# The last stage of a four-layer decoder block, the mixture of LoRA experts, as a written-out pipeline over tiles

## The chip, the cores and the metric

The kernel runs on one core of one Trainium2 chip, in one launch. The metric is the device time of an execution in microseconds (us), taken from the first to the last thing that the core does. Five engines work on it, each through its own queue of instructions: PE (TensorE, matrix products and transposes; its weight loads are listed as PEld), DVE (VectorE), ACT (ScalarE), POOL (GpSimd) and SP (SyncE, which issues most DMAs).

## What is computed

Sixteen sequences of 128 tokens with 256 channels pass through four layers. Each layer adds a gated cross attention (or a long convolution in layer 0) and then a gated feed-forward part to `x`. The change concerns the last of these eight parts, and touches the end of the one before:

```python
x = x + tanh(g_xattn[3]) * L3_xattn(layernorm(x), ctx)     # attention, 16 heads of 8
x = x + tanh(g_ffn[3])   * L3_ffn(layernorm(x))            # mixture of LoRA experts

def L3_ffn(x):                               # x: 2048 tokens x 256
    probs = softmax(x @ Wr.T + br)           # 8 experts
    expert_idx, expert_weight = argmax(probs), max(probs)
    h = einsum('nd,erd->ner', x, A)          # rank 64 for each expert
    y = einsum('ner,eor->neo', h, B) / 64
    return y[n, expert_idx] * expert_weight
```

The kernel computes `h` of all eight experts at once (8 x 64 = 512 columns), multiplies each expert's 64 columns by its gate (the probability of the best expert over 64, and zero for the seven others), and takes one product with all of `B`.

## The kernel before

`x` stays in SBUF as four tiles `xg[0..3]` of four sequences each (128 tokens on the partitions, 4 x 256 columns). A sequence is called a tile below, b = 0 to 15, and four of them are a group. The stages follow one another in `passage`, lines 1738 to 1789; each opens its own buffer pools.

Most instructions are put in order by a planner (the Tile framework), which may weave instructions of the next stage into the one before where their inputs allow. A stage under `tc.manual_schedule(engines=...)` keeps PE, DVE and ACT instructions in the order in which the program text issues them; POOL and SP follow the planner.

`stage_l3x` (the attention of layer 3, from line 1386) is such a stage: a pipeline of eight steps for a tile. On PE a tile has eight products `s` (L1568), four products `av` (L1584), eight transposes `ta` (L1600), two `tt` (L1615), the output product `y` (L1626), and for a later tile the projections `qk` (L1461, L1462) and `tv` (L1506). ACT takes the exponentials `pt` of `s` (L1575) and the scaled output `ys` (L1631). POOL adds `ys` to `x` (L1633), and for a later tile gathers two rows for each token (`yc`, L769) and takes the reciprocal root `rs` of the variance (L1443). DVE copies `av` out of PSUM (`avs`, L1595), normalises (L1607, L1610), copies `tt` (L1620), adds the gathered rows to `x` (L1432) and takes its statistics. The earlier tiles have gathers and projections for later tiles beside their own work; the last ones have none.

The softmaxes of the two attention layers are taken without subtracting a maximum. To guard this, `sums_seen` (L63, L64) keeps the largest and smallest reciprocal of a sum in `inv`. `verdict` (L66 to L80) reduces these on DVE (L70 to L73), sums over the partitions with one small PE product (L76), and writes `flag` (L78 to L80). Every engine loads the flag at the end (L48) and jumps over a second passage of the whole program, which takes the maxima and isn't executed with these inputs. `verdict` is called ahead of `stage_l3f`, with a PSUM pool of its own.

`stage_l3f` (line 1695) is left to the planner. For each group g it calls

- `layernorm` (L151): `bn_stats` and `bn_aggr` of each of four tiles on DVE (`st`, L157; `mv`, L158), `ve` (L160), the power -0.5 on POOL (`rs`, L162), and four DVE instructions `xn` (L165). The planner placed most of these statistics in `stage_l3x`, each behind the `x` of L1633 that it reads.
- `transposed` (L168): eight PE transposes (L174), the halves copied by DVE and by ACT (`xnT`, L175).
- `logits` (L343): eight small products `lg` (L347) and the addition of the bias (`l`, L354); `exp_shifted` (L357): the maximum (`mx`), the difference (`ex`, L362) and the exponential on ACT (L363).
- the sum (L1705), its reciprocal, and `topk_mask` (L327): for each pair of experts it compares "greater" (L332) and "equal" (L334), breaks ties by a constant triangle `tri` (L336), adds (L337), sums over the pairs (L339) and compares with k - 0.5 (L340). With k = 1 this marks the first of the largest. Three more instructions make `gate` (L1708 to L1710).

and then for each of the group's four tiles: `ph` (L1714, two products of 512 columns), `hid` = `ph` x `gate` on DVE (L1722), four transposes of `hid` (L1726), their copy `hT` on ACT (L1728), four products `y` (L1731), and `x` + tanh(g) x `y` on DVE (L1733). One DMA stores the group (L1734). A product of 32-bit floats is two PE instructions (passes) in the profile; a transpose is one.

Of the kernel before, what the change touches and what calls it, by code (L numbers as in the profile page):

```python
# [10 lines left out]
F32 = mybir.dt.float32  # L11
BF16 = mybir.dt.bfloat16
F32R = mybir.dt.float32r
AF = mybir.ActivationFunctionType
ALU = mybir.AluOpType
AX = mybir.AxisListType
PSUM = bass.MemoryType.PSUM

P = 128
B = 16  # L20
D = 256
NG = 4
# [33 lines left out]
def passage(ctx: ExitStack, tc: tile.TileContext, a: dict, out: bass.AP, inv, flag):  # L56
# [6 lines left out]
            nc.vector.tensor_tensor(inv[:, 0, n], inv[:, 0, n], rc, ALU.max)  # L63
            nc.vector.tensor_tensor(inv[:, 1, n], inv[:, 1, n], rc, ALU.min)  # L64

    def verdict():  # L66

        with tc.tile_pool(name="vd", bufs=1) as vd, tc.tile_pool(name="vdp", bufs=1, space=PSUM) as ps:
            m = vd.tile([P, 2, 2], F32, name="m")
            nc.vector.tensor_reduce(m[:, 0], inv[:, 0], AX.X, ALU.max)  # L70
            nc.vector.tensor_reduce(m[:, 1], inv[:, 1], AX.X, ALU.min)
            nc.vector.tensor_scalar(m[:, 0], m[:, 0], 1e20, None, ALU.is_gt)
            nc.vector.tensor_scalar(m[:, 1], m[:, 1], 1e-30, None, ALU.is_lt)  # L73
            m = m.rearrange("p a b -> p (a b)")
            t = ps.tile([1, 4], F32, name="t")
            nc.tensor.matmul(t, lhsT=ones[:, 0:1], rhs=m, start=True, stop=True)  # L76
            f = vd.tile([1, 1], F32, name="f")
            nc.vector.tensor_reduce(f, t, AX.X, ALU.max)  # L78
            nc.vector.tensor_scalar(f, f, 0.5, None, ALU.is_gt)
            nc.vector.tensor_copy(flag, f)  # L80
# [70 lines left out]
    def layernorm(pool, g, extra=None, tag="xn"):  # L151
# [12 lines left out]
        for k in range(GB):  # L164
            nc.vector.tensor_scalar(xn[:, k, :], x[:, k, :], mv[:, k, 0:1], rs[:, k : k + 1], ALU.subtract, ALU.mult)  # L165
        return xn

    def transposed(pool, ps, xn, tag="xnT"):  # L168

        xT = pool.tile([P, 2, GB * P], F32, name="xnT", tag=tag)  # L170
        for c in range(2):
            t = ps.tile([P, GB * P], F32, name="tp", tag="tp")
            for k in range(GB):
                nc.tensor.transpose(t[:, k * P : (k + 1) * P], xn[:, k, c * P : (c + 1) * P], ident)  # L174
            (nc.scalar.copy if c else nc.vector.tensor_copy)(xT[:, c, :], t)  # L175
        return xT

    def bc(ap, axis, n):

# [32 lines left out]
    def stage_l0x(ka, vbuf, anyk):  # L212

        with tc.tile_pool(name="s0", bufs=1) as s0, tc.tile_pool(name="s0w", bufs=2) as s0w, tc.tile_pool(
# [103 lines left out]
            for b in range(0, B, 2):  # L318
# [3 lines left out]
                        nc.tensor.transpose(t[:, (2 * k + c) * P : (2 * k + c + 1) * P], oT[:, c, b + k, :], ident)  # L322
                xv = xg[b // GB][:, b % GB : b % GB + 2, :].rearrange("p b d -> p (b d)")
                nc.vector.scalar_tensor_tensor(xv, t, tg[:, 0:1], xv, ALU.mult, ALU.add)


    def topk_mask(v, k, pool):  # L327

        n = v.shape[1]
        mine, other = bc(v, 3, E), bc(v, 2, E)  # L330
        gt = pool.tile([P, n, E, E], F32, name="gt", bufs=1)
        nc.vector.tensor_tensor(gt, other, mine, ALU.is_gt)  # L332
        eq = pool.tile([P, n, E, E], F32, name="eq", bufs=1)
        nc.vector.tensor_tensor(eq, other, mine, ALU.is_equal)  # L334
        f = "p t a b -> p t (a b)"
        nc.vector.tensor_tensor(eq.rearrange(f), eq.rearrange(f), bc(tri, 1, n), ALU.mult)  # L336
        nc.vector.tensor_tensor(gt.rearrange(f), gt.rearrange(f), eq.rearrange(f), ALU.add)  # L337
        m = pool.tile([P, n, E], F32, name="m")
        nc.vector.tensor_reduce(m, gt, AX.X, ALU.add)  # L339
        nc.vector.tensor_scalar(m, m, k - 0.5, None, ALU.is_lt)  # L340
        return m

    def logits(ps, xT, gw, bias=None):  # L343
        lg = ps.tile([P, GB, E], F32, name="lg", tag="tp")
        for k in range(GB):
            for c in range(2):
                nc.tensor.matmul(  # L347
                    lg[:, k, :], lhsT=xT[:, c, k * P : (k + 1) * P], rhs=gw[:, c, :], start=(c == 0), stop=(c == 1)
                )
        l = small.tile([P, GB, E], F32, name="l")  # L350
        if bias is None:
            nc.vector.tensor_copy(l, lg)
        else:
            nc.vector.tensor_tensor(l, lg, bc(bias, 1, GB), ALU.add)  # L354
        return l

    def exp_shifted(l):  # L357

        mx = small.tile([P, GB], F32, name="mx")
        nc.vector.tensor_reduce(mx, l, AX.X, ALU.max)  # L360
        ex = small.tile([P, GB, E], F32, name="ex")
        nc.vector.tensor_tensor(ex, l, bc(mx, 2, E), ALU.subtract)  # L362
        nc.scalar.activation(ex, ex, AF.Exp)  # L363
        return ex


    def moe0_weights():
# [1325 lines left out]


    def stage_l3f(wa, wb, wr, br):
        with tc.tile_pool(name="lo", bufs=2) as lo, tc.tile_pool(name="lot", bufs=2, space=PSUM) as pst, tc.tile_pool(
            name="lou", bufs=2, space=PSUM
        ) as psu:
            for g in range(NG):
                xn = layernorm(lo, g)  # L1700
                xT = transposed(lo, pst, xn)
                ex = exp_shifted(logits(pst, xT, wr, br))

                s = small.tile([P, GB], F32, name="s")
                nc.vector.tensor_reduce(s, ex, AX.X, ALU.add)  # L1705
                nc.vector.reciprocal(s, s)
                gate = small.tile([P, GB, E], F32, name="gate")
                nc.vector.tensor_tensor(gate, ex, topk_mask(ex, 1, lo), ALU.mult)  # L1708
                nc.vector.tensor_tensor(gate, gate, bc(s, 2, E), ALU.mult)
                nc.vector.tensor_scalar(gate, gate, 1.0 / 64.0, None, ALU.mult)  # L1710
                for k in range(GB):
                    ph = psu.tile([P, E, 64], F32, name="ph")
                    for c in range(2):
                        nc.tensor.matmul(  # L1714
                            ph.rearrange("p e r -> p (e r)"),
                            lhsT=xT[:, c, k * P : (k + 1) * P],
                            rhs=wa[:, c, :],
                            start=(c == 0),
                            stop=(c == 1),
                        )  # L1720
                    hid = lo.tile([P, E, 64], F32, name="hid")
                    nc.vector.tensor_tensor(hid, ph, bc(gate[:, k, :], 2, 64), ALU.mult)  # L1722
                    t = pst.tile([P, 4, P], F32, name="tp")
                    hf = hid.rearrange("p e r -> p (e r)")
                    for i in range(4):
                        nc.tensor.transpose(t[:, i, :], hf[:, i * P : (i + 1) * P], ident)  # L1726
                    hT = lo.tile([P, 4, P], F32, name="hT")
                    nc.scalar.copy(hT, t)  # L1728
                    y = psu.tile([P, D], F32, name="y")
                    for i in range(4):  # L1730
                        nc.tensor.matmul(y, lhsT=hT[:, i, :], rhs=wb[:, i, :], start=(i == 0), stop=(i == 3))  # L1731
                    xv = xg[g][:, k, :]
                    nc.vector.scalar_tensor_tensor(xv, y, tg[:, 7:8], xv, ALU.mult, ALU.add)  # L1733
                nc.sync.dma_start(out[g * GB : (g + 1) * GB].rearrange("b p d -> p b d"), xg[g])  # L1734

# [45 lines left out]
    with tc.tile_pool(name="l3fw", bufs=1) as fw:  # L1783
        l3a = col_chunks("l3a", a["L3_A"], 512, fw)
        l3B = col_chunks("l3B", a["L3_B"], D, fw)
        stage_l3x(*l3w, pos, wgt, ys)
        if not search:
            verdict()
        stage_l3f(l3a, l3B, l3r, l3br)


# [88 lines left out]
```

## Time and profile before

| | us |
|---|---|
| median of 3 runs | 1131.65 |
| lowest and highest run | 1130.06, 1133.9 |
| the profiled execution's own time | 1133.69 |
| its span, from the first to the last instruction | 1132.0 |
| PE busy in the span | 928.8 (82%) |
| DVE busy | 637.4 (56%) |
| ACT busy | 413.7 (37%) |
| POOL busy | 329.2 (29%) |
| mean granted PE clock | 0.877 |

A busy PE is not PE at its peak: where the granted clock is 0.5, the same products take twice the time. The page cuts the span into 40 slices of 28.3 us; the last four hold the end of `stage_l3x` and all of `stage_l3f`. The timeline lists instructions with start, length, engine, line, operation and names; what stands in brackets is how long the engine was idle before, and what ended that. The chain of waits is followed back from the last instruction to what released each step.

### The profile page before, as it was taken

To read this page: it belongs to the slowest core of one execution; us is meant where nothing else is said; L and a number is where in the kernel's file an instruction comes from. 1 tells how busy PE (TensorE), PEld (TensorE's weight loads), DVE (VectorE), ACT (ScalarE), POOL (GpSimd) and SP (SyncE) were. 2 spreads that over 40 slices of the span, in tenths; PEclk is the share of its full clock that TensorE was granted. 3 is DMA by queue.
4 is the path that set the end of the run, shared out by engine and by line. 5 is a ranking of instruction groups with operands and counts; after the bars stand their busy time and mean duration, and the time that the engine had idled before them with its cause. 6 is when DMAs were issued, how large, how long until landed. Compare 5 with 4: busy or idle time off the path is not lost. (4 is left out here: it accounts for less than half of the span.)

```text
span 1132.0 us, 14992 instructions
## 1 busy us (share of the span) xinstructions
PE 928.8 (82%) x5216; PEld 602.4 (53%) x5216; DVE 637.4 (56%) x1641; ACT 413.7 (37%) x674; POOL 329.2 (29%) x343
## 2 busy tenths in 40 slices
PE   3899798899998999936673658799269999998886
PEld 1444376677786454423331558688145555555563
DVE  5988847222235555389779859344245556535432
ACT  2110043233223444413331133355257777881110
POOL 5766223543034251000001117551443342210000
PEclk9999989999998999958665557899569999997998
DMA  9100170334113059000000101343388777520010
GB/s 303 26 0 1 30 198 1 93 107 100 55 56 98 29 95 116 1 29 0 1 1 0 56 19 53 97 149 95 119 234 243 201 213 197 164 66 1 19 37 22
DMA packets 71322, 94.12 MB, mean 83 GB/s; under 512 B 9191, under 2 KB 63047, under 8 KB 68935
## 3 DMA queue, kind: packets, MB, share of 16 engines
q1 hardware_dynamic: 55544, 64.98, 19.4%
q0 software_dynamic: 14080, 23.78, 10.4%
q10 hardware_dynamic: 1616, 4.33, 1.1%
q8 instruction: 45, 0.74, 0.3%
q14 instruction: 37, 0.30, 0.1%
HBM read 57.06 MB, written 33.55 MB: 80 GB/s over the span
## 5 line engine op out<-in xcount | busy, mean ns | idle before, releaser
L1575 ACT ACTIVATE pt<-s 128x1024 f32<-128x1024 f32 x128 | 126.4, 1023 | 36.7 <-PE s L1568 34.2
L769 POOL DMA_INDIRECT yc<-ys,pos x64 | 62.0, 968 | 125.9 <-DVE x L788 51.3
L309 PE MATMUL y<-kv,toep 128*128 128x512 f32 x192 | 86.7, 603 | 1.5 <-DVE toep L249 1.5
L1568 PE MATMUL s<-qa,ka 64*128 64x256 f32 x512 | 64.8, 334 | 7.3 <-ACT pt L1575 6.2
L1584 PE MATMUL av<-pt,v 128*32 128x256 f32 x1024 | 69.4, 389 | 0.1
L301 POOL TENSOR_TENSOR kv<-ctxT 128x1024 f32<-128x1024 f32 x32 | 60.1, 1899 | 28.5 <-PE y L309 28.5
L162 POOL TENSOR_TENSOR rs<-ve,neghalf 128x4 f32<-128x4 f32 x16 | 16.3, 1016 | 172.9 <-DVE ve L160 136.5
L1568 PEld LDWEIGHTS s<-qa,ka 64*128 64x128 f32 x512 | 39.0, 190 | 45.9 <-issue 24.2
L309 PEld LDWEIGHTS y<-kv,toep 128*128 128x128 f32 x192 | 35.7, 192 | 43.6 <-issue 40.2
L157 DVE BATCH_NORM_STATS2 st<-x 128x6 f32<-128x256 f32 x64 | 26.1, 415 | 52.4 <-POOL x L1633 39.8
L676 PE MATMUL ub<-L0we,xbT 128*128 x160 | 52.2, 470 | 2.6 <-ACT xbT L667 2.6
L972 PE MATMUL yb<-L2we,hT 88*128 (+1 forms) x224 | 43.0, 322 | 10.3 <-issue 4.0
L653 POOL DMA_INDIRECT xb<-xs,who x40 | 38.1, 951 | 44.9 <-PE tb L665 34.2
L907 POOL DMA_INDIRECT xb<-xs,who x40 | 38.1, 952 | 32.3 <-PE tb L919 21.0
L314 DVE TENSOR_TENSOR pr<-y,qT 128x1024 f32<-128x1024 f32 x32 | 39.0, 1222 | 12.3 <-PE y L309 9.4
L1595 DVE COPY avs<-av 128x256 f32<-128x256 f32 x64 | 26.7, 417 | 30.9 <-PE av L1584 30.7
L972 PEld LDWEIGHTS yb<-L2we,hT 88*128 88x128 f32 x224 | 34.9, 213 | 17.2 <-DVE hT L796 8.9
L537 PE MATMUL up<-L0s,xT 128*128 128x352 f32 x128 | 43.3, 484 | 0.0
L1475 POOL TENSOR_TENSOR hl<-f,hl 128x512 fp32r<-128x512 f32 x16 | 20.5, 1280 | 77.6 <-ACT hl L1474 77.6
L1147 ACT ACTIVATE pt<-s 128x1024 f32<-128x1024 f32 x32 | 32.7, 1023 | 25.4 <-PE s L1144 25.3
L317 DVE TENSOR_REDUCE oT<-pr 128x128 f32<-128x1024 f32 x32 | 38.9, 1219 | 1.0
L676 PEld LDWEIGHTS ub<-L0we,xbT 128*128 128x128 f32 x160 | 29.6, 195 | 16.2 <-ACT xbT L667 2.8
(382 smaller groups left out, 2071.6 us busy)
## 6 DMA issues: line engine op xcount, KB each, us to landing
scr<-hl SPq DMA_DIRECT2D x64, 256.0 KB
ys<-ysb SPq DMA_DIRECT2D x40, 256.0 KB
qa<-scr SPq DMA_DIRECT2D x32, 256.0 KB
ka<-scr SPq DMA_DIRECT2D x32, 256.0 KB
L2we<-in_L_w_dram POOLq DMA_DIRECT2D x6, 792.0 KB
L0we<-in_L_w_dram SPq DMA_DIRECT2D x6, 704.0 KB
xs<-xn SPq DMA_DIRECT2D x8, 512.0 KB
x<-in_x_dram SPq DMA_DIRECT2D x4, 512.0 KB
```

Of the source, the lines that this page charges most:

```text
L301: nc.gpsimd.tensor_tensor(t, bc(ch, 3, 8), bc(ch, 2, 8), ALU.mult)
L309: nc.tensor.matmul(y[:, ns], lhsT=T[:, h, d : d + P], rhs=kv[mc][:, ns], start=(mc == 0), stop=(mc == lc))
L314: nc.vector.tensor_tensor(pr, y.rearrange("p (b j i) -> p b j i", b=B, j=8), bc(qT[:, lc, :, hs], 2, 8), ALU.mult)
L317: nc.vector.tensor_reduce(oT[:, lc, :, hs], pr, AX.X, ALU.add)
L537: nc.tensor.matmul(t[:, n, 0 : 2 * I], lhsT=xT[:, c, b * P : (b + 1) * P], rhs=s13[:, c, n, :], start=(c == 0), stop=(c == 1),)
L653: nc.gpsimd.indirect_dma_start(out=xbs[s][:, i, :], out_offset=None, in_=xs, in_offset=bass.IndirectOffsetOnAxis(ap=who[:, 2 * s + i : 2 * ...
L676: nc.tensor.matmul(t[:, i, 0 : 2 * I], lhsT=xbT[:, i, c, :], rhs=we[:, bass.ds(regs[s][i] + c * 2 * I, 2 * I)], start=(c == 0), stop=(c == 1),
L769: nc.gpsimd.indirect_dma_start(out=got[b][:, i, :], out_offset=None, in_=ys, in_offset=bass.IndirectOffsetOnAxis(ap=pos[:, i, b : b + 1], ...
L972: nc.tensor.matmul(y[:, i, :], lhsT=hT[:, x, k, i, :], rhs=we[0:HI, bass.ds(at[i] + 4 * I + k * D, D)], start=(n == 0), stop=(n == 3),)
L1568: nc.tensor.matmul(s[:, h, jj, :], lhsT=ka[r, 2 * i + jj, sc * P : (sc + 1) * P], rhs=qa[r, 2 * i + jj, :], start=True, stop=True,)
L1575: nc.scalar.activation(pts[b, i][:, sc], s, AF.Exp)
L1584: nc.tensor.matmul(av[c : c + 32, :], lhsT=va[:, sc, 8 * h + 2 * i + jj, :], rhs=pt[:, sc, h, jj, :], start=(sc == 0), stop=(sc == 1),)
```

## The change

`stage_l3f` is written anew under `tc.manual_schedule`, as a pipeline with one step for each tile; its functions are issued at fixed distances ahead of the tile n of a step (`group(f, ahead)` issues once per group). The helpers `transposed`, `topk_mask`, `logits` and `exp_shifted` go. Both copies of the transposed `x` are on ACT. The mask of the best expert is now a comparison with the maximum, a running sum of the result that starts anew at every token (`tensor_tensor_scan` with `anew`, which is 0 at each first expert and 1 elsewhere), and a comparison of that sum with 1. The PSUM pools have four buffers for all but `ph`, and three for `ph`. `verdict` is called inside, in the step n = 4, and takes a PSUM buffer of the stage. `x` is stored in pairs of tiles, and the last two tiles singly.

```diff
-    def verdict():
-        with tc.tile_pool(name="vd", bufs=1) as vd, tc.tile_pool(name="vdp", bufs=1, space=PSUM) as ps:
+    def verdict(ps):
+        with tc.tile_pool(name="vd", bufs=1) as vd:
...
-            t = ps.tile([1, 4], F32, name="t")
+            t = ps.tile([1, 4], F32, name="tv", tag="a")
...
     def stage_l3f(wa, wb, wr, br):
-        with tc.tile_pool(name="lo", bufs=2) as lo, tc.tile_pool(name="lot", bufs=2, space=PSUM) as pst, tc.tile_pool(
-            name="lou", bufs=2, space=PSUM
-        ) as psu:
-            for g in range(NG):
...
+        with tc.tile_pool(name="lo", bufs=2) as lo, tc.tile_pool(name="lot", bufs=4, space=PSUM) as pst, tc.tile_pool(
+            name="lou", bufs=3, space=PSUM
+        ) as psu, tc.manual_schedule(
+            engines={mybir.EngineType.PE, mybir.EngineType.DVE, mybir.EngineType.Activation}
+        ):
+            anew = lo.tile([P, GB, E], F32, name="anew", bufs=1)
+            nc.gpsimd.memset(anew, 1.0)
+            nc.gpsimd.memset(anew[:, :, 0:1], 0.0)
...
+            def stats(g):
...
+                for k in range(GB):
+                    nc.vector.bn_stats(st[:, k, :], xg[g][:, k, :])
+                    nc.vector.bn_aggr(mv[:, k, :], st[:, k, :])
+                ve = lo.tile([P, GB], F32, name="ve")
+                nc.vector.tensor_scalar_add(ve, mv[:, :, 1], LN_EPS)
+                rs = lo.tile([P, GB], F32, name="rs")
+                nc.gpsimd.tensor_tensor(rs, ve, neghalf, ALU.pow)
+                mvs[g] = mv, rs
+
+            def normal(g):
...
+            def turn(g):
+                xn = xns.pop(g)
+                xTs[g] = lo.tile([P, 2, GB * P], F32, name="xT")
+                for c in range(2):
+                    t = pst.tile([P, GB * P], F32, name="tx", tag="a")
+                    for k in range(GB):
+                        nc.tensor.transpose(t[:, k * P : (k + 1) * P], xn[:, k, c * P : (c + 1) * P], ident)
+                    nc.scalar.copy(xTs[g][:, c, :], t)
...
+            def likely(g):
...
+                nc.vector.tensor_tensor(l, lgs.pop(g), bc(br, 1, GB), ALU.add)
...
+                nc.vector.tensor_reduce(mx, l, AX.X, ALU.max)
...
+                nc.vector.tensor_tensor(ex, l, bc(mx, 2, E), ALU.subtract)
+                nc.scalar.activation(ex, ex, AF.Exp)
+
+            def chosen(g):
...
+                nc.vector.tensor_reduce(s[:, 0], ex, AX.X, ALU.add)
+                nc.vector.tensor_reduce(s[:, 1], ex, AX.X, ALU.max)
+                nc.vector.reciprocal(s[:, 0], s[:, 0])
...
+                nc.vector.tensor_tensor(eq, ex, bc(s[:, 1], 2, E), ALU.is_equal)
...
+                nc.vector.tensor_tensor_scan(
+                    cum.rearrange(f), anew.rearrange(f), eq.rearrange(f), 0.0, ALU.mult, ALU.add
+                )
+                nc.vector.scalar_tensor_tensor(eq, cum, 1.0, eq, ALU.is_equal, ALU.mult)
+                nc.vector.tensor_tensor(ex, ex, eq, ALU.mult)
...
+                nc.vector.scalar_tensor_tensor(gate, ex, 1.0 / 64.0, bc(s[:, 0], 2, E), ALU.mult, ALU.mult)
...
+            def turn_hidden(b):
+                hf = hids.pop(b).rearrange("p e r -> p (e r)")
+                t = pst.tile([P, 4, P], F32, name="th", tag="a")
+                for i in range(4):
+                    nc.tensor.transpose(t[:, i, :], hf[:, i * P : (i + 1) * P], ident)
+                hTs[b] = lo.tile([P, 4, P], F32, name="hT")
+                nc.scalar.copy(hTs[b], t)
+
+            def down(b):
...
+                y = pst.tile([P, D], F32, name="y", tag="a")
+                for i in range(4):
+                    nc.tensor.matmul(y, lhsT=hT[:, i, :], rhs=wb[:, i, :], start=(i == 0), stop=(i == 3))
+                xv = xg[g][:, k, :]
+                nc.vector.scalar_tensor_tensor(xv, y, tg[:, 7:8], xv, ALU.mult, ALU.add)
+                if b >= B - 2:
+                    nc.sync.dma_start(out[b], xv)
+                elif k % 2:
+                    nc.sync.dma_start(out[b - 1 : b + 1].rearrange("b p d -> p b d"), xg[g][:, k - 1 : k + 1, :])
...
+            for n in range(-4, B + 2):
+
+                def group(f, ahead):
+                    g, r = divmod(n + ahead, GB)
+                    if r == 0:
+                        when(f, g, NG)
+
+                when(down, n - 2)
+                group(turn, 2)
+                group(logit, 1)
+                when(up, n)
+                when(turn_hidden, n - 1)
+                group(likely, 1)
+                group(stats, 4)
+                group(normal, 3)
+                group(chosen, 0)
+                when(gated, n)
+                if n == GB and not search:
+                    verdict(pst)
...
         stage_l3x(*l3w, pos, wgt, ys)
-        if not search:
-            verdict()
         stage_l3f(l3a, l3B, l3r, l3br)
```

`logit`, `up` and `gated` hold the same products and the same multiplication as the lines L347, L1714 and L1722 before, for one group or one tile. On PE the built program has, in a step of the steady state: `y`(n-2), the transposes `tx` or the logits `lg` of a coming group where one is due, `ph`(n), `th`(n-1), and in the step n = 4 the product `tv` of the check.

## The prediction

> **What bounds the kernel now.** I read the page's slices first, then the chain of waits in the two stages that the change can reach, then the timeline of the last one. Only the end of the span is concerned: `stage_l3x` (about 832 to 1024 us) and `stage_l3f` (1024 us to the end).
>
> ```profile
> span 1132.0 us, 14992 instructions
> ...
> PE   3899798899998999936673658799269999998886
> ...
> PEclk9999989999998999958665557899569999997998
> ```
>
> The last four slices, `stage_l3f`, read 8886 on PE: it is the bound there, with holes. The stage in one row (columns: stretch, its length, then busy time of PE, PE's weight loads, DVE, ACT and POOL, clock, DMA share, GB/s):
>
> ```profile
> 1024.00:1125.44 101.44, 87.44 (x352) 58.09 (x352) 41.23 (x115) 12.62 (x24) 1.75 (x2) 0.89 0.05 16
> ```
>
> PE is busy for 87.4 of 101.4 us, at 0.89 of its clock. The timeline gives the price of each piece of one tile, read from start to start:
>
> ```profile
> 1092.32 0.60 PE L1726 MATMUL tp<-ident,hid 128*128 128x128 f32 x4
> ...
> 1092.76 1.02 PE L1714 MATMUL ph<-l3a,xnT 128*128 128x512 f32 x2
> 1093.01 0.58 ACT L1728 COPY hT<-tp 128x512 f32<-128x512 f32 x1 [2.58 <-PE tp L1726]
> ...
> 1093.65 1.99 PE L1731 MATMUL y<-l3B,hT 128*128 128x256 f32 x8
> ...
> 1095.48 1.02 PE L1714 MATMUL ph<-l3a,xnT 128*128 128x512 f32 x2
> ```
>
> Four transposes take 0.44 us, half a `ph` (2 passes) 0.86, so a whole one 1.72, and `y` 1.83. From the first transpose to `y` it is 1.33 us, because `y` needs ACT's copy `hT`. The 0.86 of `ph` between them hides nearly all of that. Once per group the gates are late:
>
> ```profile
> 1055.17 0.19 DVE L354 TENSOR_TENSOR l<-lg,l3br 128x32 f32<-128x32 f32 x1 [0.74 <-PE lg L347]
> ...
> 1059.38 1.29 DVE L1722 TENSOR_TENSOR hid<-ph,gate 128x512 f32<-128x512 f32 x2
> 1060.13 0.42 PEld L1726 LDWEIGHTS tp<-ident,hid 128*128 128x128 f32 x4 [3.15 <-DVE hid L1722]
> 1060.13 0.66 PE L1726 MATMUL tp<-ident,hid 128*128 128x128 f32 x4 [2.32 <-DVE hid L1722]
> ```
>
> Logits to gated hidden takes 4.2 us on DVE; PE idles 2.32, and then its clock falls:
>
> ```profile
> 1060.00:1062.00 2.00, 1.87 (x6) 0.98 (x7) 0.67 (x2) 0.59 (x1) 0.00 (x0) 0.74 0.00 0
> 1062.00:1064.00 2.00, 2.00 (x6) 1.64 (x5) 0.00 (x0) 0.00 (x0) 0.00 (x0) 0.50 0.03 8
> ```
>
> In the stage before, the chain runs through work of `stage_l3f` (columns: start, length, what):
>
> ```profile
> 870.80 0.70 POOL x L1633
> 871.50 0.02 issue
> 871.52 0.43 DVE st L157
> 871.95 0.32 DVE avs L1595
> 872.27 0.32 DVE xn L1449
> 872.59 0.09 DVE mv L158
> 872.68 0.32 DVE avs L1595
> 873.00 0.05 issue
> 873.05 0.77 PE ta L1600 x5
> ```
>
> `st` (L157) is the last layernorm's statistic. DVE is held for POOL's `x`, and the `avs` that PE's `ta` needs stands behind it.
>
> [...] No scan is in this trace.
>
> **The change, part by part.** Sums are against the profiled execution, 1133.69 us with 1132.0 of span; it is 2.04 above the median of the runs, so I subtract the difference from 1131.65.
>
> *1. The statistics leave `stage_l3x`.* The written-out order keeps them together, so the planner no longer weaves `bn_stats` between the `avs`. Eight transposes `ta` take 0.82 us from first to last start where nothing holds them; in the tiles that still gather they took about 1.18 six times, 1.42 once and 2.92 once. That is 6 x 0.36 + 0.60 + 2.10 = 4.9 us. In the last of these DVE's `xn` still waits for POOL's `rs` and keeps some 0.5. I take -4.4. What is late next: tiles with gathers have a period of 12.1 us, the three that follow without gathers 11.1, with PE busy throughout. A second hole in those tiles (ACT waits 1.03 us for `s` between two `pt`) has no cause that I can name, so I leave it. Bounds: 0, if gathers and the 80% busy DMA set the period anyway; -9, if all eight tiles fall to 11.1 (7 x 1.0 + 2.2).
>
> *2. The start.* The first statistics now stand in DVE's queue between the last `avs` and `xn`, in place of the check (2.0 us, L70 to L80). Four pairs of 0.56, `ve`, and POOL's `rs` of 1.02 put `xn` at about 1025.2 instead of 1024.06. Its transposes start as each piece comes, but both copies `xT` are on ACT (0.59 each, one after the other). I get the first `ph` at 1032.0 instead of 1031.1: +0.9.
>
> *3. The tiles.* PE's order is now `y`(n-2), [group work], `ph`(n), `th`(n-1), then `y`(n-1) at once. A `y` thus follows directly on the transposes of its own tile, and the whole round through ACT is open: 1.33 - 0.44 = 0.9 us of idle PE in each tile. A step is 1.33 + 1.83 + 1.72 = 4.88 us. To it come 0.87 (8 transposes) and 1.71 (16 passes of logits at 0.107) for each of groups 1 to 3. What goes is the late gate: the mask falls from six instructions, five of about 0.42, to four small ones. The new chain costs three spacings of 0.22 before the exponential and about 1.5 us after, and is issued a step ahead of its tile. With four statistics ahead of it `hid`(8) is ready 7.5 us after `y`(6) starts; PE wants it at 8.2. The cover is 0.7 us, and without it the rest shows.
>
> Where the half clock ends is as before (about 1037): 6 passes of 0.853, two of 0.43, so `th`(0) at 1037.9, `hid`(0) at 37.5. Then `y`(0) 39.3, `y`(1) 45.0 (with 0.87), `y`(2) 51.6 (with 1.71).
>
> *4. The check inside.* At n = 4 DVE has: `stt` from 2.03 us after `y`(2)'s start, statistics of group 2 (2.4), gates of group 1 (1.5), `hid`(4) 0.69, and then four reductions and comparisons (0.6) that PE's `tv` needs 0.4 later: 7.9 us. PE reaches `tv` at 1.83 + 1.72 + 0.44 = 4.0. Behind it on PE stand `y`(3), `ph`(5) and everything else; POOL, ACT and SP wait only through these. `y`(3) starts at +8.1, not +4.88: 3.2 us. The hole of 3.9 us is longer than the one that halved the clock before, so I add 1.9 (one to two windows of 3.4 at half rate after it; bounds 1.3 and 3.1).
>
> From `y`(3) at 1059.7: 11 steps 53.7, groups 2 and 3 5.2, `y`(14) 1.83, 1.33 to `y`(15), 2.03 and 0.48 to the last sum = 64.6. End: 1124.3 + 1.9 = 1126.1, against 1125.44. So `stage_l3f` is +0.7: sixteen holes of 0.9 and one of 3.9 take the place of three late gates, three half-clock windows and the check at the start. The scan counts twice here (groups 0 and 1). Its lower bound is the 0.19 of a 128x32 row, its upper bound the 0.42 of a 128x256 row; I take 0.22[...], and keep +0.4.
>
> *5. The store.* The last transfer is 128 KB instead of 512; the earlier six pair stores and one single lie under tiles. [...] I take -0.6; bounds 0, and -1.9 (three quarters of the 2.5 us in which the last transfer's packets moved). POOL's two memsets and SP's two extra issues lie beside other work: nothing. If that cover were gone, the memsets would add about 0.3 ahead of the first `rs`, and each SP issue 0.4.
>
> Sum: -4.4 + 0.7 - 0.6 = -4.3, so 1129.4 profiled and 1127.3 in the runs.
>
> **The rivals.** *The gathers set the period* (part 1 gives nothing). For: the chain in `stage_l3x` also passes POOL's `yc` and `rs`. Against: `ta`'s holes are PE time. 1133.69 + 0.1 gives 1131.8. *All of it falls to PE's 11.1 us.* For: PE's holes are small in the tiles without gathers. Against: the 1.03 us hole. -9 + 0.1: 1122.8. *Slower: the half clock comes back tile after tile.* Place: the 0.9 us hole in each step. Price: a window of 3.4 us at half rate costs 1.7. It decides from the third extra window; from five (+8.5) the end is 1135.8. For: the row of PEclk falls to 5 in stages with holes. Against: at 1097 the profile shows two holes of 0.79 and 0.29 close together, and the clock stayed. That the change doesn't do what it says is no rival: the built order has the pieces where I put them.
>
> **How the numbers follow.** Forecast 0.50 (1127.3, own range 1124 to 1130.5); gathers 0.18 (1131.8); PE's floor 0.15 (1122.8); half clock 0.17 (1135.8). 0.3% is 3.4 us, about what can be told from no change. Faster, below 1128.3: three quarters of the forecast and the floor, 0.53. Slower, above 1135.0: the half clock and a fifth of the gathers case (with a dear scan and a long half clock after the check), 0.21. The rest, 0.26, is within. Range 1121.5 to 1136.5: it leaves out the far ends of the floor (0.05) and of the half clock (0.10).
>
> **What would show it.** `ta` at 0.82 us in all tiles and a period of about 11.7 instead of 12.1 in `stage_l3x`; a wait of about 0.9 us of PE's `y` weight load for `hT` in each of 16 tiles; PE idle for 3 to 5 us ahead of `tv`, with half clock after it; no wait of `th` for `hid` except in the first group. The forecast is wrong if the period stays 12.1, if `y` doesn't wait, or if DVE is also late at n = 8 and 12.

## The result, and the profile after

The changed kernel takes 1125.76 us (median of 20 runs, 1122.84 to 1131.19), the kernel before 1130.57 (20 runs on the same chip). The ratio is 0.9955 with a 95% interval of 0.9939 to 0.9971: 5.1 us faster, between 3.3 and 6.9. The profiled execution of the changed kernel took 1125.45 us, about its median; that of the kernel before took 1133.69, 3 us above its own, so the two traces lie further apart (8.3 us of span) than the runs.

The page after, with the same three lines as before:

```profile
span 1123.7 us, 14998 instructions
...
PE   3899798899998999937763567899259999998886
...
PEclk9999989999999999967775557899669999997999
```

The last four slices of PE still read 8886, but the clock of the last three is 9 throughout. The last stage in one row (same columns as before):

```profile
1018.02:1117.64 99.62, 83.31 (x355) 56.94 (x354) 38.62 (x126) 14.96 (x29) 4.74 (x5) 0.94 0.06 21
```

PE is busy for 83.3 of 99.6 us, at 0.94 of its clock instead of 0.89: fewer us of busy time because less of it is at half rate, and more idle time between.

I cut both traces at four events that each has once: the first transpose `ta` of tile 0 and of tile 15 in the attention, the first `y` of the last stage, and the end of its last sum. The starts come from the timeline.

| stretch | before | after | difference | predicted |
|---|---|---|---|---|
| start to `ta` of tile 0 | 848.51 | 846.53 | -1.98 | none |
| to `ta` of tile 15 (attention) | 170.86 | 166.85 | -4.01 | -4.4 |
| to the first `y` | 19.53 | 19.59 | +0.06 | +0.4 |
| to the end of the last sum | 86.55 | 84.67 | -1.88 | +0.3 |
| to the end of the span | 6.51 | 6.08 | -0.43 | -0.6 |

The first row is not the change's: nothing it touches runs there. The rest sums to -6.3, inside the interval of the runs.

In the attention the statistic is gone from the chain, and a new break stands in it. The chain of waits around one tile (columns: start, length, what):

```profile
867.51 0.91 PE s L1518 x4
...
868.44 1.03 ACT pt L1525
...
869.52 0.50 PE s L1518 x4
870.02 1.02 PE ta L1550 x8
```

All eight `ta` are one piece of 1.02 us, with no `st` or `avs` ahead of them. They take 0.82 us from first to last start in 14 tiles (1.65 in tile 4, where DVE's `xn` still waits for POOL's `rs`, and 1.11 in the last). The period with gathers, from a tile's first `ta` to the next tile's, is 11.7, as forecast. But `pt` starts almost 1 us late; that is taken up below.

In the last stage, the timeline of one step (start, length, engine, line, what; the bracket is idle time and what ended it):

```profile
1085.15 0.59 ACT L1750 COPY hT<-th 128x512 f32<-128x512 f32 x1 [1.57 <-PE th L1748]
...
1085.79 1.99 PE L1757 MATMUL y<-l3B,hT 128*128 128x256 f32 x8 [0.73 <-ACT hT L1750]
...
1087.62 1.85 PE L1691 MATMUL lg<-l3r,xT 128*128 128x8 f32 x16
...
1089.32 1.96 PE L1731 MATMUL ph<-l3a,xT 128*128 128x512 f32 x4
...
1091.12 0.60 PE L1748 MATMUL th<-ident,hid 128*128 128x128 f32 x4
...
1092.45 0.48 PE L1757 MATMUL y<-l3B,hT 128*128 128x256 f32 x1 [0.73 <-ACT hT L1750]
```

`y` waits for `hT` in fifteen of the sixteen tiles, 0.67 to 0.73 us each time; `y`(3) stands behind the check's product and finds its `hT` ready. `th` waits for `hid` only in the first tile, 0.2 us. From `y` to `y` it is 4.88 us in a plain step, 5.75 with `tx` and 6.66 with `lg`. The check, at n = 4:

```profile
1048.88 0.60 PE L1748 MATMUL th<-ident,hid 128*128 128x128 f32 x4
...
1050.10 0.18 DVE L1713 TENSOR_REDUCE s<-ex 128x4 f32<-128x32 f32 x1
...
1050.63 0.22 DVE L1719 TENSOR_TENSOR_SCAN cum<-anew,eq 128x32 f32<-128x32 f32 x1
...
1051.63 0.69 DVE L1742 TENSOR_TENSOR hid<-ph,gate 128x512 f32<-128x512 f32 x1
...
1052.55 0.17 DVE L73 TENSOR_SCALAR m<-m 128x2 f32<-128x2 f32 x1
...
1052.86 0.19 PE L76 MATMUL tv<-m,ones 128*1 128x4 f32 x2 [3.38 <-DVE m L73]
```

PE stands for 3.38 us until DVE has been through statistics, gates, `hid` and the four instructions of the check. Yet the clock stays at 1.00 after it.

### The profile page after: what moved, and what is told of

Its sections match the earlier page's. It is cut to its first block, busy times and chain, and to the rows that moved or that the text cites. A ratio compares the mean times of both kernels' runs of the same rounds, so it can differ in the third digit from the quotient of the medians.

```text
span 1123.7 us, 14998 instructions
## 1 busy us (share of the span) xinstructions
PE 919.9 (82%) x5216; PEld 597.8 (53%) x5216; DVE 631.8 (56%) x1625; ACT 415.5 (37%) x678; POOL 329.7 (29%) x345
## 5 line engine op out<-in xcount | busy, mean ns | idle before, releaser
L162 POOL TENSOR_TENSOR rs<-ve,neghalf 128x4 f32<-128x4 f32 x12 | 12.2, 1015 | 157.6 <-DVE ve L160 121.5
L1757 PE MATMUL y<-l3B,hT 128*128 128x256 f32 x128 | 31.9, 392 | 10.8 <-ACT hT L1750 10.8
```

## The experiments

They ran in three later sessions, each on a chip of its own and beside the kernel before on the same chip (medians 1122.07, 1119.99 and 1119.84 there). The chip of the first runs isn't named with their results; that it was a fourth one, called the first chip below, is inferred from its times. Ratios are to the runs of the same chip; differences between kernels are best read from the stretches of each trace, which repeat closely where no half clock comes in (the attention without the statistics: 162.52 to 162.63 us in nine traces). "Half clock" is the time at 0.5 from the first `y` to the last sum.

| run | ratio (95%) | attention | to first `y` | to last sum | half clock |
|---|---|---|---|---|---|
| kernel before, again | 1.0009 (0.9996 to 1.0021) | 170.83 | 19.63 | 85.00 | 6.8 |
| changed kernel, again | 0.9939 (0.9920 to 0.9959) | 162.57 | 19.11 | 86.29 | 3.4 |
| before, new mask alone | 0.9928 (0.9907 to 0.9949) | 170.87 | 18.03 | 76.69 | 0 |
| before, statistics kept out | 0.9939 (0.9918 to 0.9959) | 162.57 | 20.85 | 86.54 | 10.2 |
| before, both | 0.9852 (0.9830 to 0.9873) | 162.52 | 19.17 | 76.70 | 0 |
| changed, check split | 0.9888 (0.9868 to 0.9908) | 162.59 | 19.79 | 81.90 | 0 |
| changed, `th` ahead of `ph` | 0.9835 (0.9811 to 0.9859) | 162.62 | 21.71 | 75.64 | 6.8 |
| changed, statistics back | 0.9945 (0.9926 to 0.9964) | 170.44 | 17.28 | 82.40 | 0 |
| changed, statistics in idle time | 0.9876 (0.9851 to 0.9901) | 162.59 | 14.63 | 82.40 | 0 |
| changed, old mask | 0.9980 (0.9970 to 0.9991) | 162.57 | 20.96 | 90.00 | 6.8 |
| changed, three edits | 0.9759 (0.9739 to 0.9779) | 162.59 | 18.66 | 69.47 | 0 |
| same, more statistics moved | 0.9777 (0.9753 to 0.9800) | 162.63 | 16.01 | 68.08 | 0 |

**Both kernels once more.** No edit.

> The kernel before unaltered, for a trace beside the others on their chip. Theory A (the period with the statistics is 12.1 on every chip, since it is set by the round of POOL's sum, the statistic behind it and the copies behind that): 12.1, with transposes of 1.8 us rather than 1.2 where the changed kernel's period is 11.1; 86.5 us from the first y to the last sum, with three windows of half clock. Rival (the first chip's attention is slower in both kernels): 11.5.

> The changed kernel unaltered, once more, beside other kernels and perhaps on another chip. Theory A (the half clock after a hole depends on where the hole falls in the windows of 3.4 us): the hole ahead of the check's product is 3.4 us again, and a window of half clock follows it or not; the last stage takes 84.7 us from the first y to the last sum without one, 86.4 with one. Theory B (the attention's period without the statistics differs from chip to chip: 11.7 us in the first trace of the changed kernel, 11.1 in two experiments of the call before): period 11.1 to 11.7, and against the kernel before a gain of 5 us at 11.7 and of 9 to 10 us at 11.1. Rival to B (the period belongs to the code, and those experiments changed it): 11.7.

The period with the statistics was 12.1 again, with transposes of 1.8 us. Without them it was 11.1 here and in every other run that keeps them out. So the statistics cost 170.83 - 162.57 = 8.3 us on these chips, and 4.0 on the first. Against the kernel before, the changed kernel gained 6.8 us here (4.6 to 9.0 by the interval), less than the 9 to 10 that I expected at a period of 11.1; and the kernel before had two windows of half clock behind its late gates, not three. The chain of waits of the kernel before, on the new chip:

```profile
862.29 0.71 POOL x L1633
863.00 0.02 issue
863.02 0.43 DVE st L157
863.45 0.32 DVE avs L1595
863.77 0.32 DVE xn L1449
864.09 0.09 DVE mv L158
864.18 0.32 DVE avs L1595
864.50 0.04 issue
864.55 0.76 PE ta L1600 x5
```

It is the chain that the prediction started from, instruction for instruction. What differs between the two sessions is another hole. The same stretch of the changed kernel on the first chip (first fence) and on this one (second), 10.75 us apart:

```profile
866.88 0.94 POOL L719 DMA_INDIRECT yc<-ys,pos  x1 [0.30 <-issue]
867.18 0.83 PE L1518 MATMUL s<-qa,ka 64*128 64x256 f32 x6
...
867.65 0.42 DVE L1545 COPY avs<-av 128x256 f32<-128x256 f32 x1 [1.49 <-PE s L1518]
...
868.44 1.02 ACT L1525 ACTIVATE pt<-s 128x1024 f32<-128x1024 f32 x1 [0.98 <-PE s L1518]
```

```profile
855.68 4.14 ACT L1525 ACTIVATE pt<-s 128x1024 f32<-128x1024 f32 x4
856.13 0.95 POOL L719 DMA_INDIRECT yc<-ys,pos  x1 [0.30 <-DMA scr<-hl]
...
856.34 0.42 DVE L1545 COPY avs<-av 128x256 f32<-128x256 f32 x1 [0.94 <-PE av L1534]
```

POOL's gather starts at the same moment of the tile in both. On the first chip DVE's `avs` then comes 0.56 us later, and ACT has a hole of 0.98 us between two `pt`; on the second ACT runs through four `pt` without one. The periods (11.7 and 11.1) differ by the same 0.6 us. Both traces of the first chip have the hole, and none of the twelve traces of the others has it at this place. Why the two engines start late there isn't settled; no run here tests it, and since each chip was seen in one session only, chip and session can't be told apart.

The trace of the changed kernel also had its half clock this time, after the same 3.38 us hole. In these traces the half clock comes in windows of 3.41 us whose edges lie on one grid: in the first trace of the kernel before it starts at 1060.95, 1084.85 and 1108.74 us, seven windows apart each time, while the holes that it follows are 24.25 us apart. The first of these windows and the one ahead of it:

```profile
1057.54:1060.95 3.41, 1.09 (x6) 0.69 (x6) 2.86 (x8) 0.07 (x1) 0.00 (x0) 1.00 0.00 0
1060.95:1064.37 3.42, 3.42 (x8) 2.21 (x7) 0.00 (x0) 0.52 (x1) 0.00 (x0) 0.50 0.02 5
```

At half clock one pass of `ph` follows another after 0.85 us (the kernel before, 1033.0 to 1035.5), otherwise after 0.43. Rows of the changed kernel cut at such edges, first the original trace, then this one:

```profile
1047.73:1051.14 3.41, 1.75 (x8) 0.74 (x6) 3.14 (x17) 0.59 (x1) 0.81 (x1) 1.00 0.00 0
1051.14:1054.55 3.41, 1.69 (x9) 1.53 (x10) 1.87 (x10) 0.00 (x0) 0.20 (x1) 1.00 0.01 2
```

```profile
1034.63:1038.04 3.41, 0.10 (x2) 0.11 (x2) 2.85 (x16) 0.58 (x1) 1.01 (x1) 0.99 0.00 0
1038.04:1041.45 3.41, 3.41 (x10) 2.74 (x9) 0.43 (x3) 0.00 (x0) 0.00 (x0) 0.51 0.01 2
```

In the first trace the hole was cut in two by an edge: each window kept half of its PE time (1.75 and 1.69 of 3.41), and the clock stayed. In the second it filled one window (0.10 busy), and the next ran at 0.5. From `y`(3) to `y`(4) it was 6.50 us instead of 4.88: the half clock cost 1.6 us in this trace and nothing in the other, and what differs is where the hole falls.

**The mask alone, in the kernel before.**

```diff
-                nc.vector.tensor_tensor(gate, ex, topk_mask(ex, 1, lo), ALU.mult)
-                nc.vector.tensor_tensor(gate, gate, bc(s, 2, E), ALU.mult)
-                nc.vector.tensor_scalar(gate, gate, 1.0 / 64.0, None, ALU.mult)
+                nc.vector.tensor_reduce(top, ex, AX.X, ALU.max)
+                nc.vector.tensor_tensor(eq, ex, bc(top, 2, E), ALU.is_equal)
+                nc.vector.tensor_tensor_scan(
+                    cum.rearrange(f), anew.rearrange(f), eq.rearrange(f), 0.0, ALU.mult, ALU.add
+                )
+                nc.vector.scalar_tensor_tensor(eq, cum, 1.0, eq, ALU.is_equal, ALU.mult)
+                nc.vector.tensor_tensor(ex, ex, eq, ALU.mult)
+                nc.vector.scalar_tensor_tensor(gate, ex, 1.0 / 64.0, bc(s, 2, E), ALU.mult, ALU.mult)
```

> The kernel before with one part of the change alone: the mask by the running sum (and the shorter gate) in place of the comparison of all pairs. The order of PE's instructions is the same. Theory A (the late gate is what the rewritten stage gained): the span from the logits to the gated hidden falls from 4.2 to about 2.7 us in each of four groups, PE's hole ahead of the first transposes of a group falls from 2.3 to about 0.8, and the three windows of half clock that followed these holes (1.7 us each) are gone: 9 to 11 us faster, about 1120. Theory B (the half clock stays): 6 us faster, about 1124.5. Theory C (the gate's wait is replaced by another one, so the change's gain in the last stage comes from elsewhere): within 2 us of 1130.6.

Theory A. The timeline at the start of a group:

```profile
1058.65 1.02 PE L1726 MATMUL ph<-l3a,xnT 128*128 128x512 f32 x2
1060.45 0.66 PE L1738 MATMUL tp<-ident,hid 128*128 128x128 f32 x4 [0.78 <-DVE hid L1734]
...
1061.84 1.99 PE L1743 MATMUL y<-l3B,hT 128*128 128x256 f32 x8 [0.29 <-ACT hT L1740]
```

The late gate's hole is 0.78 us instead of 2.32, and no window of half clock is left. By the ratio the gain is 8.1 us (5.7 to 10.4), a little less than the 9 to 11 that I expected. From the first `y` to the last sum it is 76.69 us: 8.3 to 9.9 us less than the kernel before (85.00 and 86.55), and 8.0 less than the changed kernel (84.67). Six DVE instructions in place of nine did more for this stage than the whole change.

**The statistics alone, and both parts, in the kernel before.** All of `st` lies in one tile here, which a DVE memset writes when the attention's last tile begins.

```diff
+    st_all = cst.tile([P, B, 6], F32, name="st_all")
...
-                xn = layernorm(lo, g)
+                xn = layernorm(lo, g, st=st_all[:, g * GB : (g + 1) * GB])
...
                 b, u = divmod(n, 8)
+                if n == 8 * B and not search:
+                    nc.vector.memset(st_all, 0.0)
```

> The kernel before with one part of the change alone: the last layernorm's statistics (and POOL's roots of them) no longer stand among the attention's instructions; one DVE memset late in the attention, which they must follow, keeps them out. PE's order is the same. Theory A (my part 1): the eight transposes of a tile take 0.82 us instead of 1.18 to 2.92, the period with gathers is 11.7 instead of 12.1, and the attention is 4.0 us shorter; the last stage has 0.6 to 2.4 us more, since its DVE takes the statistics now: 1.5 to 3.5 us faster in all, about 1128. Rival (the gathers set the period, and the shorter attention of the changed kernel has another cause): period 12.1, and the whole is equal or up to 2 us slower.

> The kernel before with two parts of the change and without its rewritten order: the mask by the running sum, and the statistics kept out of the attention by one memset. Theory A (these two parts hold all of the change's gain, and the rewritten order gives some of it back): 8 us in the attention and 9.9 in the last stage, less 1.3 for the statistics at the start: 16 to 17 us faster than the kernel before, so 7 to 9 us faster than the changed kernel. Rival (the parts share one gain): 11 us or less.

With the statistics out, the attention took 162.57 us and `ta` 0.82: the whole 8.3 us, more than the 4.0 that I expected from the first chip. The start gives 1.2 back. With the mask as well the ratio is 0.9852 against 0.9928 and 0.9939 for either: the two gains add up. That kernel keeps the planner's order and is about 0.9% faster than the changed one.

**The statistics put back, and put where DVE is idle.** `stat` and `aggr` are the `bn_stats` and `bn_aggr` of tiles 0 to 11; the last stage takes those of the others.

```diff
-                    ((begin, 4), (rsqrt, 3), (keep_values, -1, 2), (spread, 2)),
-                    ((normal, 3), (clear, 3)),
+                    ((begin, 4), (rsqrt, 3), (stat, -2), (keep_values, -1, 2), (spread, 2)),
+                    ((normal, 3), (clear, 3), (aggr, -2)),
```

> The changed kernel with the statistics of tiles 0 to 11 put back into the attention's DVE order at exactly the places that they had in the kernel before; POOL's roots of them stay in the last stage. Theory A (my part 1: the statistic waits for POOL's sum, and the copies that PE's transposes need stand behind it): the transposes take 1.2 to 1.8 us in eight tiles, the period is 12.1, the attention 2.5 to 8 us longer (4.0 where the changed kernel's period is 11.7, 7 to 8 where it is 11.1); the last stage is 2.8 us shorter, since the hole ahead of the check loses 2.2 us of statistics and the start 0.6. In all 1.2 us slower than the changed kernel at 11.7, about 5 slower at 11.1. Rival (it was POOL's roots, moved along with the statistics, that held the attention): no longer transposes, and 2.8 us faster than the changed kernel.

```diff
-                    ((keep_turned, -1, 0), (keep_turned, -1, 1)),
+                    ((keep_turned, -1, 0), (keep_turned, -1, 1), (stat, -2), (aggr, -2)),
```

> As the run with the statistics put back, but placed five steps of the tile later, behind the two copies oT, where POOL's sum has long been written and DVE is idle for 1.1 us; the work on DVE is the same. Theory A (only the wait for POOL's sum costs, not the 0.56 us of work): transposes of 0.82 us, the changed kernel's period, and the last stage 2.8 us shorter: 2.8 us faster than the changed kernel. Rival (DVE's work as such lengthens the tile): 4 us or more slower than theory A.

Put back, they cost 170.44 - 162.57 = 7.9 us, with transposes of 1.8 us; POOL's roots, which stayed in the last stage, are cleared. Placed five steps later, the same work costs nothing (162.59). DVE in one tile of that run:

```profile
873.74 0.49 DVE L1581 COPY oT<-tt 128x128 f32<-128x128 f32 x2 [0.24 <-PE tt L1576]
874.15 0.42 DVE L92 BATCH_NORM_STATS2 st_all<-x 128x6 f32<-128x256 f32 x1
874.60 0.18 DVE L96 BATCH_NORM_AGGREGATE mv_all<-st_all 128x2 f32<-128x6 f32 x1
875.31 0.42 DVE L1556 COPY avs<-av 128x256 f32<-128x256 f32 x1 [0.53 <-PE av L1545]
```

`st` no longer waits (its bracket is gone), and `avs` still waits for PE, not PE for `avs`. It is the wait that cost, not the 0.56 us of work. Both whole times miss what I expected: put back, the kernel is as fast as the changed one (ratios 0.9945 and 0.9939, where I had 5 us slower), and with the statistics in idle time it is 7.1 us faster by the ratios (3.5 to 10.6), not 2.8. The reason is the last stage, which was shorter than I expected in both runs: 2.3 us of the hole ahead of `tv` went, as forecast, and with it the half clock after it; and at the start PE stood idle for less time, so that the first `y` came 1.8 us earlier in the first run and 4.5 us in the second, which had one window of half clock (3.4 us) there in place of three.

**The check split.** `extremes` issues the four DVE instructions of L70 to L73, `verdict` the product `tv` and what follows it.

```diff
-                if n == GB and not search:
-                    verdict(pst)
+                if n == GB + 1 and not search:
+                    m = extremes()
+                if n == GB + 2 and not search:
+                    verdict(pst, m)
```

> The changed kernel, with the check's four DVE reductions issued at the end of step 5 and its PE product in step 6, so that the product finds its input ready. Theory A (the check stands in PE's way for its hole alone): the 3.4 us hole ahead of the product goes, the distance from the third to the fourth y falls from 7.65 to 4.88 us: 2.8 us faster than the changed kernel, about 1123. Theory B (in most executions the half clock follows the hole, and the profiled one escaped it): 4.0 to 4.7 us faster in the median, about 1121.5. Rival: the DVE is late for the next gated hidden anyway, and the wait moves there: less than 1 us.

From the third to the fourth `y` it is 4.88 us, and from the first `y` to the last sum 81.90: 2.77 less than 84.67, theory A to the hundredth. Theory B isn't excluded: the changed kernel's second trace had the half clock too. By the ratios (0.9888 and 0.9939, on two chips) the gain is 5.7 us with an uncertainty of about 3.

**`th` ahead of `ph`.**

```diff
-                when(up, n)
                 when(turn_hidden, n - 1)
+                when(up, n)
```

> The changed kernel with two calls of a step exchanged, so that PE's order is y(n-2), group work, th(n-1), ph(n), y(n-1): the ph lies in the round of th through ACT. Theory A (my part 3, the round is open by 0.73 to 0.9 us in each tile): 14 rounds of 0.89 us closed, a hole of about 1.2 us ahead of th(8), because its gated hidden comes behind four statistics, and 0.4 at the start: about 10 us faster than the changed kernel, about 1115.5. Rival 1 (th now waits for the gated hidden in each tile): no more than 4 us. Rival 2 (the wait shows because PE is at its floor in this stage, and the records of its ends mislead): within 1 us.

Theory A, 11.6 us faster than the changed kernel by the ratios (8 to 15): a plain step is 3.88 us instead of 4.88, and the stretch 75.64 instead of 86.29, in spite of two windows of half clock behind the check. The hole ahead of th(8) is there, 5.27 - 3.88 = 1.4 us.

**The old mask in the changed kernel.** The six instructions of `topk_mask` and three for the gate stand in `chosen`.

> The changed kernel with the mask of the kernel before (the comparison of all pairs) and its three gate instructions. The chain from the exponential to the gated hidden is 3.3 us then instead of 1.5. Theory A (my part 3: the mask is hidden behind a whole step of other work except where the DVE is late): the hole ahead of the check's product grows from 3.4 to 5.1 us, one of 0.4 comes ahead of th(8), and 1.2 at the start: 3.4 us slower than the changed kernel, up to 5 with a further window of half clock. Rival (the mask is worth in the rewritten order what it is worth in the old one, where it alone shortened the last stage by 9.9 us): 8 to 10 us slower.

Theory A. The step with the check grew by 1.9 us (9.52 against 7.64), the step ahead of th(8) by 0.5, and a second window of half clock came: 90.00 against 86.29. The rewritten order hides most of a slower mask, as it hides most of the gain of a faster one.

**All together.** Check split, `th` first, statistics in idle time; then the statistics of tiles 12 to 14 moved likewise.

> The changed kernel with three edits together: th ahead of ph, the check's reductions issued a step ahead of its product, and the statistics of tiles 0 to 11 behind the copies oT of the attention. Theory A (the waits that these edits take away are all that PE has in the last stage): y follows y after 3.88 us, 4.76 and 5.62 where group work lies between, and 3.06 at the end; 67.7 us from the first y to the last sum instead of 84.7, no half clock: 17 us faster than the changed kernel, and the fastest of all. Rival (what one edit gains the others gain too, or DVE becomes the bound): 11 us or less.

> The run with the three edits together, with the statistics of tiles 12 to 14 placed in the attention's idle DVE time too. Theory A (the one hole left in its steady state, 1.4 us ahead of th(8), is DVE's, behind four statistics): the hole goes, 68.1 us from the first y to the last sum instead of 69.5, 1.4 us faster than that run. Rival (that hole has another cause): the same time.

The first took 69.47 us from the first `y` to the last sum. It misses my 67.7 by 1.4 us ahead of th(8), which I had seen in the run before and not carried over, and by some 0.3 around the check. The second took 68.08: the hole was DVE's. In the runs the two can't be told apart (0.9759 and 0.9777, with overlapping intervals). PE in the second has no wait left in the steady state (one of 0.73 us remains ahead of the last `y`):

```profile
1040.29 0.19 PE L77 MATMUL tv<-m,ones 128*1 128x4 f32 x2
1040.41 2.00 PE L1776 MATMUL y<-l3B,hT 128*128 128x256 f32 x8
1042.24 1.85 PE L1710 MATMUL lg<-l3r,xT 128*128 128x8 f32 x16
1043.95 0.64 PE L1767 MATMUL th<-ident,hid 128*128 128x128 f32 x4
1044.42 1.88 PE L1750 MATMUL ph<-l3a,xT 128*128 128x512 f32 x4
1046.14 1.89 PE L1776 MATMUL y<-l3B,hT 128*128 128x256 f32 x8
```

Both are 25 to 27 us faster than the kernel before, and 18 to 20 faster than the changed one.

## Why the prediction was right, point by point

**The statistics (part 1): right in mechanism and, on that chip, in size.** -4.0 against -4.4, with `ta` at 0.82 and the period at 11.7. The runs with the statistics put back and put in idle time show the mechanism: a wait for POOL's sum in DVE's queue, with `avs` behind it. The case "all of it falls to PE's 11.1 us" came true too for the attention, on three other chips: 8.3 us. What I left as "a second hole that has no cause that I can name" decides between the two; its cause is still open. That the forecast's -4.4 fits the first chip and not the others is therefore luck in part: it left that hole alone without knowing what makes it. The rival "the gathers set the period" fell: the period moved as soon as the statistics left.

**The start (part 2): the direction was right.** The first `xn` came 0.8 us later relative to the attention (forecast 1.1), the first `ph` 0.6 (forecast 0.9). By the first `y` nothing of it was left (+0.06 against +0.4). The half clock ended at an edge of its own, 0.4 us earlier relative to the attention, which by my estimate (half of it) gives back 0.2; the rest isn't taken apart. Much of this stretch is half clock, one window in the shortest run and five in the longest: over the runs it lies between 14.6 and 21.7 us.

**The tiles (part 3): right to the hundredth.** 4.88 us a step, 0.87 for `tx`, a `y` that waits for `hT` in fifteen tiles. (With `lg` a step is 6.66, 0.07 more than the sum.) Exchanging two lines removes the bubble and 1.00 us from each plain step. The scan took 0.224 us where I had put 0.22, my estimate between two bounds; a `tensor_tensor` of that size takes 0.19. My sentence that no scan is in the trace is wrong; the earlier stages of the kernel before have ten:

```profile
L439 DVE TENSOR_TENSOR_SCAN cum<-ce,eq x4: 424/425/425, 168.4 to 672.2; 128x128 f32<-128x128 f32 x4
...
L465 DVE TENSOR_TENSOR_SCAN be<-ones,nb x2: 174/174/175, 173.6 to 677.7; 128x8 f32<-128x8 f32 x2
```

A straight line through these two sizes gives 0.224 us for 32 elements, with no need of bounds; and the scan of 128 elements takes what a `tensor_tensor` of 256 takes (0.42). The cover of 0.7 us that I gave the new mask at n = 8 is about 1.3: `hid`(8) was ready 7.0 us after `y`(6) started, not 7.5, and PE came to it at 8.4, not 8.2 (4.88 + 1.83 + 1.72). The old mask, 1.87 us longer in its run, shows 0.5 there.

**The check (part 4): the hole was right, the half clock after it was the term that I mis-sized.** 3.38 us of hole against 3.9, and `y`(3) 2.8 us late against 3.2. (The terms that I listed for DVE give 7.6 us, or 8.0 with `stt`'s own 0.40, not 7.9; it took 7.5, mostly because `tv` started 0.14 us after the last comparison and not 0.4.) The 1.9 us of half clock cost 0 in the profiled execution and 1.6 in another of the same kernel. I took the hole's length as what decides. It isn't: 2.32 us were enough five times of six in the two traces of the kernel before, and 3.38 us were enough in one trace of the changed kernel and not in the other. In this stretch it went with how much of one window of the clock the hole empties, and the windows didn't follow the holes: in the first trace of the kernel before the half clock starts seven windows of 3.41 us apart, where the holes lie 24.25 us apart. This term is 1.9 of the 2.2 us between +0.3 and -1.9 in the last stage.

**The store (part 5):** -0.43 against -0.6, which was my estimate. The size fits, and the tail is shorter in every trace that stores `x` in pairs (5.93 to 6.17 us against 6.49 to 6.58). That the smaller transfer makes it so is not shown; no run changes the store alone.

**Faster or slower.** The sum had the right sign because its largest term did. That the medians fell by 4.8 us where I forecast 4.3 is closer than the parts deserve: on this chip they add up to -6.3 in the traces, 1.9 of it half clock that I had forecast and that didn't come, and on other chips the attention alone gave 8.3. The slower rival, half clock tile after tile, fell: in the steady state of the changed kernel's first trace PE is busy for at least 2.68 us of a window of 3.41, and none followed. What the prediction did not draw out is how the last stage's account is made up: the mask alone is worth 8 to 10 us in it, and the written-out order returns nearly all of that as fifteen bubbles and the check's hole.

## What to carry to other kernels

Of an instruction that waits for another engine, ask what stands behind it in its queue: the same statistic cost 8 us ahead of the copies that PE needs and nothing five steps later. In an order written out by hand, don't let a product follow directly on the transposes whose copy it needs where another tile's product can stand between: with `ph` there a plain step took 3.88 us here, without it 4.88. A change that mixes several edits is best taken apart first: here one part alone (the mask, 0.9928) is worth as much as the whole, and two lines exchanged are worth more (0.9835 against 0.9939).

## What the runs showed of the hardware

- A clock window of 3.4 us with 1.09 us of PE records (32%) was followed by half clock in all five cases looked at in the two traces of the kernel before; so was one with 1.23 us (36%) in the run with `th` ahead of `ph` (1031.28 to 1034.69). One with 1.42 us (42%), after a hole of 2.32 us as well, was not, nor those with 1.69 and 1.75 us. The rows of the kernel before, on the other chip:

```profile
1048.34:1051.75 3.41, 1.09 (x4) 0.22 (x2) 3.07 (x10) 0.00 (x0) 0.00 (x0) 1.00 0.00 0
...
1072.23:1075.65 3.42, 1.42 (x4) 0.35 (x2) 3.08 (x11) 0.00 (x0) 0.00 (x0) 1.00 0.00 0
```

- The busy share of these records is no general rule. At the end of the attention, in the changed kernel's first trace, a window with 1.70 us was followed by half clock, though one with 1.69 us behind the check was not; in the kernel before even one with 2.16 us was (1020.00 to 1023.41). What the clock counts stays open.

```profile
1013.60:1017.01 3.41, 1.70 (x10) 0.90 (x8) 3.19 (x18) 0.00 (x0) 0.17 (x2) 1.00 0.00 0
1017.01:1020.43 3.42, 2.05 (x5) 0.90 (x5) 2.21 (x7) 0.56 (x1) 1.90 (x2) 0.50 0.00 0
```

- The same kernel differs between sessions by more than the change is worth: the kernel before has medians of 1130.57, 1122.07, 1119.99 and 1119.84 us in four sessions, the last three on three different chips. Most of it lies ahead of the part that is studied here (the first `ta` at 848.5 and 840.0 us in its two traces). Ratios here are therefore taken within one chip and session.
